# The attention steps of a fused conv-attention kernel: rows turned behind the normalised stream, the feed-forward product as four column tiles, the turn of the maxima ahead of the output product

## The chip, the cores and the metric

The kernel runs on one core of a Trainium2 chip. Its engines are TensorE (PE in the profile, with PEld for its weight loads), VectorE (DVE), ScalarE (ACT), GpSimd (POOL) and SyncE (SP), which issues most DMAs. They run their own instruction streams and wait for each other by semaphores. The metric is the device time of one execution in microseconds (us); the median of some runs is given, and one execution was recorded by the hardware profiler.

## The reference

The input x is 16 images of 64 x 64 positions with 128 channels (f32). One layer of three parts follows: a two-dimensional gated recurrence over the normalised image, an attention of the Nystrom kind over the 4096 positions of an image (8 heads of 16 channels, 64 landmarks), and a feed-forward recurrence along the positions. The part that matters here is the attention, with the first product of the feed-forward part:

```python
q_l = q.reshape(b, h, m, l, dh).mean(axis=3)          # landmarks: means over 64 positions
k_l = k.reshape(b, h, m, l, dh).mean(axis=3)
attn1 = softmax(q @ k_l.T); attn2 = softmax(q_l @ k_l.T); attn3 = softmax(q_l @ k.T)
out = attn1 @ pinv(attn2) @ (attn3 @ v) + conv33(v)
t = t + x + out @ w_out + b_out                       # x is the normalised stream
Wx = layer_norm(t) @ W.T                              # first product of the feed-forward part
```

(The lines are shortened; softmax, the 33-tap convolution along the positions and the pseudo-inverse are the reference's.)

## The kernel before, in words

The program has a stage of statistics, the two-dimensional recurrence (to about 1700 us of the span), the attention (to about 3400 us) and the feed-forward recurrence. Only the attention is touched.

**Tiling.** The attention works on groups of 512 positions: 8 groups make an image (Q = 8), 16 images make 128 groups. A group is 4 chunks of 128 positions (C = 4). One call of `step(s)` moves a software pipeline by one group: it handles different stages of groups that lie up to 20 apart. `new` is group s: its keys, values and queries are projected (L979, copied by ScalarE at L987, L997, L1007) and its scores against the landmark queries are taken (`greatest`, L1028), of which VectorE finds the maxima (`keep_greatest`, L1032, from bank 3 down to bank 0). `after` is group s + 1: the rows of the normalised stream are turned on TensorE into channels by positions (`turn_rows`, L960 on the tile at_xh) and copied by ScalarE (`keep_rows`, L968). `mid` is group s - 8, for which the weights against the landmark queries are made (`weigh`, L1058 and L1064; `weights`, L1073) and summed (`add_weights`, L1100 on GpSimd; `attend_values`, L1080). `first` is group s - 15: scores against the landmark keys (`compare`, L1135), their maxima (`topmost`, L1143), split into three bf16 parts by GpSimd (`part_top`, L1151 to L1154), turned (`turn_top`, L1159), copied (`keep_top`, L1163), and then used in `soften` (L1170 for the shift by the maxima, L1172 for the scores). `cur` is group s - 16: exponentials (`softened`, L1177), `attend` (L1184), the convolution (`convolve`, L1107), and `divide`: two transposes on VectorE (L1193), a reciprocal into PSUM (L1195) and a multiplication (L1197). `third` is group s - 17: output product (`output`, L1212) and sum (`keep_sum`, L1216). `fourth`, s - 18: mean and variance (`measure`, a statistics instruction L1225 and an aggregation L1226 for each chunk) and factors (on GpSimd). `fifth`, s - 19: normalised stream (`normalise`, L1238), its turn (`turn_output`, L960 on at_z, copied at L975), the feed-forward product (`feed`, L1244) and its copy, which also reorders the positions (`keep_feed`, L1248). `sixth`, s - 20: its statistics (L1252).

`step` runs for s = 15 to 127. Earlier steps have their own functions, and so have the steps after the last group (`last_step`); these are not changed. The first step of an image (`start`) has more to do: it gathers the sums of the image before and spreads its values.

**PSUM.** The results of TensorE go to PSUM, of which the program uses eight pieces of 512 f32 numbers in each partition, called banks. Six have numbers (`bank(k, ...)`, `banks(...)`), two are handed out as a pair. A bank has one tile at a time: an instruction that writes a new tile into a bank waits until the readers of the tile before are done. The numbers matter for the change: keys and `greatest` use bank 0, values bank 1, `greatest` banks 0 to 3, `weigh` 4, 5 and the pair, `turn_top` 2, `output` 3, `turn_output` 1, `attend` 4 and 5, the reciprocals of `divide` 2, `feed` 3, `turn_rows` 4, `attend_values` 5, `soften` 0 to 3, `compare` 4, 5 and the pair.

**Order.** In the attention the order on TensorE, VectorE, ScalarE and GpSimd is written out by hand (`tc.manual_schedule`): each engine executes in the order in which the functions of `step` are called. SP's queue of DMAs is ordered by the program's scheduler. Between the projection of the queries and the end of a step, the order of the calls is that of the diff below.

**Shapes of TensorE.** The profile gives a matmul's tile as rows x columns. The array can work as one tile of 128*128, as four tiles of 128*32 (four products for different columns of the output run side by side), of 32*128 (four products over different rows), or as eight of 64*32. `product` makes four products of 32 columns when `apart` is set:

```python
def product(out, lhsT, rhs, apart):
    for r in map(quarter, range(NP)) if apart else (slice(0, P),):
        nc.tensor.matmul(out[r], lhsT[:, r], rhs, start=True, stop=True)
```

An f32 product is two matmuls in the trace, one pass after the other.

Of the kernel before, what the change touches and what calls it, by code (L numbers as in the profile page):

```python
# [14 lines left out]
P = 128  # L15
# [830 lines left out]
def attention(nc, tc, t1, gamma, beta, wqkv, ident, mhalf, fixed, xp, rows, qm, km, pinvT, vd, t2, wx, wx_stats, out, ahead):  # L846
# [14 lines left out]
    C = 4  # L861
# [4 lines left out]
    BF = mybir.dt.bfloat16  # L866
    with ExitStack() as ctx:
# [7 lines left out]
        def bank(k, shape, dtype=F32):  # L875
            return ps.tile(shape, dtype, tag=f"bank{k}", name=f"at_bank{k}")
# [63 lines left out]
        def carry_factors(gr):  # L940
            gr.nbt = nb = sm.tile([P, 2, C], F32, tag="nb", name="at_nb")
            nc.gpsimd.tensor_tensor(nb[:, 1], gr.T[:, :, F], gr.T[:, :, F + 2], ALU.mult)
            nc.gpsimd.tensor_scalar(nb[:, 0], gr.T[:, :, F + 2], 1.0, None, ALU.add)
# [29 lines left out]
        def keep_output(gr):  # L973
            gr.zT = wk.tile([P, GC], F32, tag="zT", name="at_zT")
            nc.scalar.copy(gr.zT, gr.pz)  # L975
# [177 lines left out]
            nc.gpsimd.tensor_copy(top[:, :, 2:4], mx)  # L1153
            nc.gpsimd.tensor_tensor(top[:, :, 4:6], mx, top[:, :, 2:4], ALU.subtract)  # L1154

        def turn_top(gr):
            gr.pt = bank(2, [P, C, P], BF)
            for c in range(C):
                nc.tensor.transpose(gr.pt[:, c, :], gr.top[:, :, :, c].rearrange("p n s -> p (n s)"), ident_b)  # L1159

# [48 lines left out]
        def output(gr, k=3):  # L1209
            gr.po = bank(k, [P, C, F])  # L1210
            for c in range(C):
                nc.tensor.matmul(gr.po[:, c, :], gr.oT[:, c * P : (c + 1) * P], wo, start=True, stop=True)  # L1212
# [26 lines left out]
                    gr.z[:, c, :], gr.u[:, c, :], AF.Identity, bias=gr.nb[:, c : c + 1], scale=gr.r3[:, c : c + 1]  # L1239
                )  # L1240

        def feed(gr, k=3):
            (gr.pf,) = banks(k)
            nc.tensor.matmul(gr.pf, wfT, gr.zT, start=True, stop=True)  # L1244

        def keep_feed(gr):
            gr.fx = fx = wk.tile([P, GC], F32, tag="fx", name="at_fx")
# [152 lines left out]
        def step(s):  # L1400
            b, q = divmod(s, Q)
            new, after, mid, was = group(s), group(s + 1), group(s - Q), group(s - Q - 1)
            first, cur, third, fourth, fifth, sixth = (group(s - 2 * Q + d) for d in (1, 0, -1, -2, -3, -4))
            start = q == 0
            if first:
                compare(first)
            if cur:
                softened(cur)
            project_keys(new, apart=not start)
            if start:  # L1410
                sums(mid.im)
            project_values(new, apart=not start)
            if s == 2 * Q - 1:
                attend_values(was, 3)
                keep_values(was)
            if first:
                topmost(first)
            if sixth:
                measure_feed(sixth)
            if fourth:  # L1420
                measure(fourth, (0,))
            keep_keys(new)
            keep_projected(new)
            project_queries(new, apart=not start)
            if start and was:
                gather(was.im)
            if fourth:
                measure(fourth, (1,))
            keep_queries(new)
            if start:  # L1430
                turn_split(mid.im)
            if fifth:
                normalise(fifth)
            greatest(new)
            if first:
                carry_factors(first)
                carry(first, 2, nc.gpsimd)
            weigh(mid)
            keep_greatest(new)
            if first:  # L1440
                part_top(first)
            if third:
                output(third)
            weights(mid)
            if first:
                carry(first, 3, nc.gpsimd)
            if start and was:
                spread_values(was.im)
            if first:
                turn_top(first)  # L1450
            if fifth:
                turn_output(fifth)
                keep_output(fifth)
            if third:
                keep_sum(third)
            if fourth:
                measure(fourth, (2, 3))
            if cur:
                attend(cur)
            if first:  # L1460
                keep_top(first)
            add_weights(mid, (3, 1, 0), mid.g == 0)
            if fourth:
                factors(fourth)
            add_weights(mid, (2,))
            if q == Q - 1:
                shift(new.im)
            if cur:
                convolve(cur, pair())
                divide(cur)  # L1470
            if fifth:
                feed(fifth)
            if after:
                turn_rows(after)
            if fifth:
                keep_feed(fifth)
            if after:
                keep_rows(after)
            if first:
                carry(first, 0, nc.scalar)  # L1480
            attend_values(mid)
            if cur:
                add_convolved(cur)
            keep_values(mid)
            if first:
                soften(first)
                carry(first, 1, nc.scalar)
                carry_bias(first)
            if cur:
                turn_attended(cur)  # L1490
            fetch(s)
# [345 lines left out]
```

## Time and profile before

| What | us |
|---|---|
| median of 3 runs (lowest, highest) | 3635.04 (3631.91, 3635.63) |
| the profiled execution: its time, its span | 3638.43, 3636.9 |
| an ordinary step of the attention | 12.69 |
| the first step of an image | 15.79 |
| in the stretch 2400 to 2600: TensorE, VectorE, ScalarE, GpSimd busy of 200 | 199.1, 174.7, 163.2, 153.5 |

Times in the profile count from the first instruction. A step's length is the distance of the same instruction in two steps in a row. In the lists of instructions in order of time, a row merges instructions of a kind that follow each other: its first number is the start of the first, its second the time to the end of the last; the bracket, where there is one, gives idle time of the engine before it and what ended it. A matmul's end is modelled, and it is drawn with the time that its data takes through the array, so two matmuls in a row overlap; the distance of their starts is what one costs.

### The profile page before, as it was taken

Reading aid. Unit: us, or ns where it says so; the run is one execution under the profiler, and the core shown is the slowest. Engines: PE = TensorE matmul, PEld = TensorE weight load, DVE = VectorE, ACT = ScalarE, POOL = GpSimd, SP = SyncE. Lnnn points to the kernel's source line nnn. Section 1 sums busy time; section 2 is a strip of 40 time slices with the busy share of each in tenths; the row PEclk is TensorE's granted clock in tenths of the full one; section 3 lists DMA queues with packets and bytes.
Section 4 is the critical chain, followed back from the end, with each engine's and each line's share of the span. In section 5 each row is a group of like instructions: output and inputs, shape, how many; then the busy total and the mean of one; then the engine's idle time right before and its main releaser. Section 6 shows DMA issues by size and latency. Waiting matters only on the chain. (4 is left out here: it accounts for less than half of the span.)

```text
span 3636.9 us, 106193 instructions
## 1 busy us (share of the span) xinstructions
PE 3499.9 (96%) x40438; PEld 2343.7 (64%) x40438; DVE 2982.8 (82%) x7005; ACT 2499.9 (69%) x5126; POOL 2489.2 (68%) x3843
## 2 busy tenths in 40 slices
PE   7899999999999998999999999999999999997988
PEld 5666665545567666985666666666666666654777
DVE  8699999998889887544888888888888888888665
ACT  0466556656667665445788888888888888876787
POOL 1577877777788885434777777777777777785223
PEclk9999999999999999999999999999999999999999
DMA  9223232333333321023677777777777777667799
GB/s 339 83 76 80 80 86 80 84 84 83 85 88 86 81 76 38 4 63 92 147 185 187 164 162 163 166 167 163 164 166 166 165 164 168 157 143 187 201 273 182
DMA packets 834210, 484.50 MB, mean 133 GB/s; under 512 B 304672, under 2 KB 800672, under 8 KB 833696
## 3 DMA queue, kind: packets, MB, share of 16 engines
q1 hardware_dynamic: 814026, 442.55, 47.8%
q0 software_dynamic: 17728, 34.61, 5.3%
q8 instruction: 322, 5.28, 0.6%
q14 instruction: 192, 1.57, 0.1%
q10 hardware_dynamic: 1942, 0.50, 0.1%
HBM read 239.21 MB, written 238.29 MB: 131 GB/s over the span
## 5 line engine op out<-in xcount | busy, mean ns | idle before, releaser
L1100 POOL TENSOR_TENSOR at_total<-at_total,at_e 128x512 f32<-128x512 f32 x472 | 603.1, 1278 | 228.3 <-ACT at_e L1073 208.6
L290 ACT ACTIVATE ls_g<-ls_z,ls_b 128x304 f32<-128x304 f32 (+26 forms) x950 | 494.0, 545 | 225.0 <-PE ls_z L288 192.7
L283 PE MATMUL ls_z<-ls_xn,ls_w 128*128 128x432 f32 (+28 forms) x1700 | 586.1, 492 | 1.5 <-POOL ls_xn L275 1.2
L283 PEld LDWEIGHTS ls_z<-ls_xn,ls_w 128*128 128x128 f32 x1700 | 309.6, 191 | 189.4 <-issue 98.1
L288 PE MATMUL ls_z<-ls_hsum,ls_u 128*128 128x304 f32 (+26 forms) x1140 | 369.7, 461 | 0.0
L1032 DVE TENSOR_REDUCE at_mxq<-at_bank 128x1 f32<-128x512 f32 x512 | 314.9, 677 | 53.0 <-PE at_bank L1028 53.0
L323 POOL TENSOR_TENSOR ls_tt<-ls_ve,mhalf 128x8 f32<-128x8 f32 (+2 forms) x190 | 312.7, 1646 | 19.8 <-DVE ls_ve L322 4.2
L288 PEld LDWEIGHTS ls_z<-ls_hsum,ls_u 128*128 128x128 f32 x1140 | 211.6, 194 | 128.6 <-issue 78.4
L1177 ACT ACTIVATE at_eT<-at_bank 128x512 f32<-128x512 f32 x512 | 264.5, 604 | 42.1 <-PE at_bank L1172 41.5
L406 ACT ACTIVATE ls_g<-ls_cell 128x304 f32<-128x304 f32 (+26 forms) x190 | 93.2, 491 | 268.1 <-DVE ls_cell L405 267.8
L288 PE MATMUL ls_z<-ls_h,ls_u 128*128 128x304 f32 (+26 forms) x760 | 256.2, 460 | 12.3 <-DVE ls_h L410 12.3
L402 POOL TENSOR_TENSOR ls_g<-ls_g,ls_cell 128x304 f32<-128x304 f32 (+26 forms) x190 | 180.1, 948 | 127.7 <-ACT ls_g L290 113.0
L340 ACT ACTIVATE ls_tt<-ls_tt,ls_nb 128x128 f32<-128x128 f32 (+9 forms) x632 | 261.0, 478 | 5.6 <-POOL ls_tt L323 5.0
L979 PE MATMUL at_bank<-at_xT,wqkv 128*32 128x512 f32 (+1 forms) x1684 | 262.8, 602 | 2.0 <-DVE at_cmx L1143 1.1
L275 POOL TENSOR_TENSOR ls_xn<-ls_xn,grstd 128x272 f32<-128x272 f32 (+40 forms) x186 | 209.9, 1129 | 76.2 <-DVE ls_xn L270 71.2
L1143 DVE TENSOR_REDUCE at_cmx<-at_bank 128x8 f32<-128x512 f32 x256 | 175.6, 686 | 103.8 <-PE at_pair L1135 102.1
L1248 ACT COPY at_fx<-at_bank 128x512 f32<-128x512 f32 x128 | 133.7, 1044 | 142.9 <-PE at_bank L1244 138.3
L1619 DVE SCALAR_TENSOR_TENSOR rc_y<-rc_w,rc_scale,rc_z 128x256 f32<-128x256 f32 x344 | 154.6, 481 | 86.3 <-PE rc_z L1606 84.5
L1238 ACT ACTIVATE at_z<-at_u,at_nb,at_r 128x128 f32<-128x128 f32 x512 | 209.6, 484 | 4.6 <-POOL at_nb L1233 4.5
L288 PEld LDWEIGHTS ls_z<-ls_h,ls_u 128*128 128x128 f32 x760 | 141.9, 193 | 107.8 <-issue 53.2
L1600 POOL DMA_DIRECT2D out_dram<-rc_tt x64 | 77.4, 1209 | 168.4 <-ACT rc_tt L1597 145.0
L1193 DVE STREAM_TRANSPOSE at_t<-at_bank 128x512 f32<-128x512 f32 x256 | 167.9, 695 | 25.3 <-PE at_bank L1184 25.2
(281 smaller groups left out, 9683.8 us busy)
## 6 DMA issues: line engine op xcount, KB each, us to landing
at_win<-vd SPq DMA_DIRECT2D x256, 256.0 KB
t<-ls_tt SPq DMA_DIRECT2D x392, 130.0 KB
at_T<-t SPq DMA_DIRECT2D x128, 264.0 KB
gs_xb<-in_x_dram SPq DMA_DIRECT2D x64, 512.0 KB
at_xh<-t SPq DMA_DIRECT2D x128, 256.0 KB
vd<-at_v SPq DMA_DIRECT2D x128, 256.0 KB
t<-at_u SPq DMA_DIRECT2D x128, 256.0 KB
out_dram<-at_u SPq DMA_DIRECT2D x128, 256.0 KB
```

The costliest lines, as they stand in the source:

```text
L275: eng.tensor_tensor(a, a, norm(v, grstd), ALU.mult)
L283: nc.tensor.matmul(v.z[g][:, : v.total], wt[g], v.xn[:, : v.total], start=True, stop=True)
L288: nc.tensor.matmul(view(v, v.first.z[g]), ut[g], hin, start=False, stop=True, skip_group_check=True)
L290: nc.scalar.activation(a[:, : v.cols], z, AF.Tanh if g == 4 else AF.Sigmoid, bias=bt[g])
L323: nc.gpsimd.tensor_tensor(v.tt[:, 0:k, F + 2 : F + 4], ve[:, :, :k].rearrange("p r k -> p k r"), mhalf[:, : 2 * k].rearrange("p (k r) -> p ...
L340: nc.scalar.activation(v.tt[:q, k, F + 4 :], v.tt[:q, k, 0:F], AF.Identity, bias=v.nb[:q, k : k + 1], scale=v.tt[:q, k, F + 3 : F + 4],)
L402: nc.gpsimd.tensor_mul(v.a[1], v.a[1], v.cl)
L979: nc.tensor.matmul(out[r], lhsT[:, r], rhs, start=True, stop=True)
L1032: nc.vector.tensor_reduce(gr.im.mxq[:, n : n + 1, gr.g], gr.s[n], AX.X, ALU.max)
L1100: eng.tensor_tensor(total, total, e[:, :, c, :], ALU.add)
L1177: nc.scalar.activation(gr.eT[:, n], gr.s[n], AF.Exp)
L1238: nc.scalar.activation(gr.z[:, c, :], gr.u[:, c, :], AF.Identity, bias=gr.nb[:, c : c + 1], scale=gr.r3[:, c : c + 1])
```

## The change

In `step`, for all steps unless the condition says otherwise:

- `turn_rows(after)` goes ahead of `keep_sum(third)` and `attend(cur)`, directly behind `turn_output(fifth)`, and takes bank 0 instead of 4. `keep_rows(after)` goes behind `keep_top(first)`, ahead of `keep_feed(fifth)`.
- `feed(fifth)` makes four products of 32 columns instead of one of 128, still in bank 3.
- `part_top(first)` goes ahead of three other GpSimd operations of the same group.
- In steps that are not the first of an image: `turn_top(first)` goes ahead of `output(third)`; it takes bank 3, and the output bank 2. The statistics of chunk 1 of `fourth` go from ahead of the maxima (`keep_greatest`) to behind the output's sum (`keep_sum`).

No operation is added or left out but for the feed's products, of which there are four narrow ones in place of one.

```diff
-        def turn_top(gr):
-            gr.pt = bank(2, [P, C, P], BF)
+        def turn_top(gr, k=2):
+            gr.pt = bank(k, [P, C, P], BF)
...
-        def feed(gr, k=3):
+        def feed(gr, k=3, apart=False):
             (gr.pf,) = banks(k)
-            nc.tensor.matmul(gr.pf, wfT, gr.zT, start=True, stop=True)
+            product(gr.pf, wfT, gr.zT, apart)
...
-            if fourth:
+            if fourth and start:
                 measure(fourth, (1,))
             keep_queries(new)
...
             greatest(new)
             if first:
+                part_top(first)
                 carry_factors(first)
                 carry(first, 2, nc.gpsimd)
             weigh(mid)
             keep_greatest(new)
-            if first:
-                part_top(first)
+            if first and not start:
+                turn_top(first, 3)
             if third:
-                output(third)
+                output(third, 3 if start else 2)
             weights(mid)
...
-            if first:
+            if first and start:
                 turn_top(first)
             if fifth:
                 turn_output(fifth)
                 keep_output(fifth)
+            if after:
+                turn_rows(after, 0)
             if third:
                 keep_sum(third)
             if fourth:
-                measure(fourth, (2, 3))
+                measure(fourth, (2, 3) if start else (1, 2, 3))
             if cur:
                 attend(cur)
             if first:
                 keep_top(first)
+            if after:
+                keep_rows(after)
             add_weights(mid, (3, 1, 0), mid.g == 0)
...
                 convolve(cur, pair())
                 divide(cur)
             if fifth:
-                feed(fifth)
-            if after:
-                turn_rows(after)
-            if fifth:
+                feed(fifth, apart=True)
                 keep_feed(fifth)
-            if after:
-                keep_rows(after)
             if first:
                 carry(first, 0, nc.scalar)
             attend_values(mid)
```

## The prediction

> **What bounds the kernel now.** I read the page's header and its table of 40 slices first, then the busy time of the stretch in which the changed code runs, then the order of single instructions over one step, and last two steps in which the same order happens to be disturbed.
>
> ```profile
> span 3636.9 us, 106193 instructions
> PE 3499.9 (96%) x40438; PEld 2343.7 (64%) x40438; DVE 2982.8 (82%) x7005; ACT 2499.9 (69%) x5126; POOL 2489.2 (68%) x3843
> 1776.21:3175.93 1399.72, 1393.33 (x23629) 910.34 (x23627) 1222.77 (x2621) 1146.30 (x2274) 1083.55 (x1898) 1.00 0.72 167
> ```
>
> The third line is the stretch of the full attention steps: TensorE (first number after the length) is busy for 1393.33 of 1399.72 us at the full granted clock, VectorE for 1223. So a step's length is TensorE's: 12.69 us in the ordinary steps, 15.79 in the first step of an image. Whether a shorter TensorE program shortens the step depends on what comes ready just in time for it. One ordinary step, from the output product on (start, duration):
>
> ```profile
> 2411.83 1.16 PE L1212 MATMUL at_bank<-at_wo,at_oT 128*128 128x128 f32 x8
> 2412.83 0.39 PE L1159 MATMUL at_bank<-at_identb,at_top 128*128 128x128 bf16 x4
> 2413.05 0.61 PE L960 MATMUL at_bank<-ident,at_z 128*128 128x128 f32 x4
> 2413.58 1.09 PE L1184 MATMUL at_bank<-at_eT,at_g 64*32 64x512 f32 x16
> 2414.47 0.64 PE L1107 MATMUL at_pair<-at_win,bands 64*32 64x256 f32 x16
> 2414.76 1.31 DVE L1193 STREAM_TRANSPOSE at_t<-at_bank 128x512 f32<-128x512 f32 x2
> 2415.03 1.12 PE L1244 MATMUL at_bank<-at_zT,at_wfT 128*128 128x512 f32 x2
> 2416.00 0.60 PE L960 MATMUL at_bank<-ident,at_xh 128*128 128x128 f32 x4
> 2416.18 0.36 DVE L1195 RECIPROCAL at_bank<-at_t 128x32 f32<-128x32 f32 x1
> 2416.20 1.05 ACT L1248 COPY at_fx<-at_bank 128x512 f32<-128x512 f32 x1 [1.17 <-PE at_bank L1244]
> 2416.53 1.08 PE L1080 MATMUL at_bank<-at_e,at_v 128*32 128x128 f32 x32
> 2416.58 0.69 DVE L1197 TENSOR_TENSOR at_m<-at_t,at_bank 128x512 f32<-128x512 f32 x1
> 2417.54 0.40 PE L1170 MATMUL at_bank<-at_topT,at_minus 32*128 32x512 bf16 x4
> ```
>
> The reader is to see a race between `attend` (L1184) and `soften` (L1170). TensorE needs 3.96 us for it (2413.58 to 2417.54): attend, convolution, feed, the turn of the rows, values. Meanwhile VectorE must turn attend's two banks (L1193), take reciprocals into bank 2 (L1195) and multiply by them (L1197, end 2417.26), because the third product of L1170 writes bank 2. ScalarE must empty bank 3 (L1248, end 2417.24) for the fourth. VectorE's chain is 1.18 from attend's start to L1193, then 2.50 to the end of L1197, and 0.05 for the release: 3.73 us. Its margin to TensorE is only 0.23. What happens without the margin is shown by the last step, which has no rows left to turn:
>
> ```profile
> 3184.66 1.09 PE L1184 MATMUL at_bank<-at_eT,at_g 64*32 64x512 f32 x16
> 3185.84 1.31 DVE L1193 STREAM_TRANSPOSE at_t<-at_bank 128x512 f32<-128x512 f32 x2
> 3187.21 0.81 PEld L1080 LDWEIGHTS at_bank<-at_e,at_v 128*32 128x32 f32 x32 [0.80 <-DVE at_t L1193]
> 3187.66 0.69 DVE L1197 TENSOR_TENSOR at_m<-at_t,at_bank 128x512 f32<-128x512 f32 x1
> 3188.23 0.56 PE L1170 MATMUL at_bank<-at_topT,at_minus 32*128 32x512 bf16 x4
> ```
>
> There the values wait for L1193 to leave bank 5, and the four products of L1170 stretch over 0.56 instead of 0.40: the third starts at 3188.40, 0.05 after L1197 ends and again 3.73 after attend's start. That is the order of the changed kernel between attend and soften. A second disturbance: at 2430.23 the reciprocal came 0.35 late, the third product 0.12 later than its usual 0.007 behind the first, and that step became 12.84 us long instead of 12.69. So a late bank 2 goes into the step in full, and 0.03 on top (the four row tiles of soften run on out of step).
>
> **Part 1, turn_rows ahead of attend (bank 0).** Four transposes at 0.109 us apart, 0.437 in all, leave the path from attend to soften and stand between the turn of the stream and attend. On TensorE alone this is neutral or better: both turns are 128x128, so one change of tile shape goes. But attend starts 0.437 later, and with it VectorE's chain. New cover: none. Bank 0 is read last by the maxima (L1032), which end at about 2413.33; the turn is due at 2413.49, so it does not wait. Its copy (`keep_rows`, 0.77) moves into ScalarE's idle 1.17 before L1248 and is free; its reader is the next step's keys. The rows' load for a later group is issued earlier on SP; the buffers are two to three steps ahead, so I count nothing.
>
> **Part 2, the feed as four tiles of 32 columns, beside the values of the same shape.** From single instructions: after the last L1107 (2414.73, 0.21 long) the next weights start 0.09 after it has streamed, and L1244's two passes start 0.53 apart where 0.43 is the streaming, so 0.10 of weight load is exposed. Another 0.09 and 0.03 stand between the turn of the rows and L1080. The keys (L979, already apart) show 0.45 between their passes, and no gap follows where values and queries keep that shape. The saving is 0.10 - 0.02 + 0.09 + 0.01, about 0.18 us a step: TensorE alone would need 12.51. All of it lies between attend and soften, where TensorE then waits: its own way is 1.45 to the feed, 0.88 for it, 0.91 for the values, 0.09 for the change: 3.33 against VectorE's 3.73. So part 2 is worth nothing here. ScalarE's copy of the feed is next: the feed's last pass starts at attend + 1.92, L1248 follows 0.63 behind (2415.57 to 2416.20 now) and takes 1.05: end at 3.60, bank 3 free at 3.66, just inside 3.73.
>
> The row that the new order leans on is L1248: 1.05 us to empty one bank, however its product is made. The Trainium skill, TensorEngine Tiling (Array Packing), section Key Properties, says that changing the tiling mode drains the engine; that fits the 0.09 gaps. The same page, section PSUM Bottleneck, says that tiling speeds up the products but not the emptying of PSUM, which may become the limit; that speaks against this change. By the first rule alone the kernel would gain 0.18 x 109, some 20 us; by the second it gains none of that.
>
> **Part 3, the turn of the maxima ahead of the output product, banks 2 and 3 swapped.** The same twelve matmuls; the engine still changes shape once before them. Before, L1212's first weight load is exposed by 0.107 (0.213 between its first two starts, 0.11 later); now the bf16 load is exposed and half of the f32 load behind a 0.055 transpose: 0.055 + 0.05. I take 0, and bound it by all hidden and both exposed: -0.11 to +0.11. `part_top` moves ahead of three GpSimd operations and ends near 2411.07, before its turn at 2411.83. [...]
>
> **Part 4, measure 1 behind the output's sum.** VectorE's first maximum starts at 2410.92 now. L1028's last pass starts at 2410.20, and 0.68 (as from attend's last pass, 2414.08, to L1193) gives 2410.88: 0.04 sooner, no more. The output's last product starts at 2412.94 instead of 2412.71, so its sum (L1216) stays at 2413.3; three statistics of 0.41 behind 0.60 end at about 2415.12, where attend is ready for L1193 at 2415.20. Hidden, by 0.08.
>
> **The sum.** From soften's third product to the next attend is 8.73 us now. New step: 8.73 + 0.437 + 0.03 + 3.73 = 12.93, against 12.69: **+0.237 us**. Feed and rows both exist in 108 steps (numbers 19 to 126): +25.6 us. Of the steps before, the one whose soften starts at 1750.97 is already waiting (0.44), and the next has 0.34 to spare (0.10): +0.5. The first steps of images show the same margin (0.23) and are counted alike. The profiled execution, 3638.4 (span 3636.9), becomes 3664.5; it lies 3.4 over the median of the runs, 3635.04, so I forecast 3661 for the median. With part 3's bounds: 0.13 to 0.344 a step, 3650 to 3673.
>
> **Rivals.**
> - Faster: TensorE's program alone sets the step, -0.18 x 109 = -20 us, 3615. It needs VectorE's chain from attend to be 0.4 us shorter than 3.73, or bank 2 not needed; the last step speaks against it. TensorE's busy share and the removed shape change speak for it. It decides from the point where L1197 ends ahead of attend + 3.3.
> - No change: the late products of soften are made up behind it, or the maxima's turn saves its full 0.11 and the queue of weight loads another 0.1: 3635 to 3642. The disturbance at 2430 speaks against it.
> - Slower still: the three statistics end last, not attend. The added one is 0.41 to 0.46 and hidden by 0.08 only; with a sum that comes 0.1 to 0.2 later, 11 to 22 us come on top: 3672 to 3683. Two rows here speak for a close call, none for a later sum.
>
> **Chances.** Forecast 0.75 (3650 to 3673), slower still 0.09, no change 0.07, faster 0.09. The range 3642 to 3674 leaves the faster case, most of the slowest and half of no change out. By 0.2% (7.3 us, about what a measurement of this kernel can tell from no change): faster 0.09, same 0.07, slower 0.84.
>
> **What will show it.** Right: ordinary steps of about 12.93; L1193 starting 1.18 after attend; weight loads of L1080 waiting for DVE at_t; the third product of L1170 0.05 after L1197 and 0.15 to 0.2 behind the first; TensorE's busy time down by some 20 us while the span grows. Wrong: steps of 12.5 with L1170's four products within 0.02 (faster); L1193 with VectorE never idle before it and more than 1.25 after attend (slower still); an idle gap before the turn of the rows from L1032 (bank 0 late, a cost that I hold to be none).

## The result, and the profile after

| | before | after |
|---|---|---|
| median of 5 runs (lowest, highest), us | 3635.63 (3631.91, 3637.67) | 3671.18 (3670.26, 3676.87) |
| the profiled execution: its time, its span | 3638.43, 3636.9 | 3671.96, 3670.5 |
| ordinary step of the attention | 12.69 | 13.00 |
| first step of an image | 15.79 | 15.96 |

The ratio of the medians is 1.0099, with a 95% interval of 1.0086 to 1.0112: the changed kernel is slower by about 36 us. The forecast was 3661, its range 3642 to 3674. The direction and the place held, and so did the cause, VectorE's chain behind a later `attend`; which of its releases holds a step is less simple than the prediction had it (below). The forecast step was 0.07 us too short (12.93 for 13.00), and over the steps this is most of the 10 us by which the forecast missed.

The first two lines are the head of the page and its table of engines, for the changed kernel:

```profile
span 3670.5 us, 107432 instructions
PE 3525.2 (96%) x41092; PEld 2332.9 (64%) x41092; DVE 2994.0 (82%) x7005; ACT 2503.8 (68%) x5126; POOL 2491.3 (68%) x3843
```

TensorE's share is 96%, as before. By this line alone TensorE would look as busy as ever, and 25 us busier in sum, although by the prediction's estimate its program became shorter; the step below shows where its waits are hidden. The table of waits names them (engine and line that waited, for whom; us in total, times, longest):

```profile
PEld at_bank L1080 <- DVE at_t L1193: 110.0, 113, 1.6
ACT at_eT L1177 <- PE at_bank L1172: 84.1, 120, 3.2
DVE at_mxq L1032 <- PE at_bank L1028: 79.5, 127, 8.4
```

Before, no wait of L1080 stood among the thirty longest. Now the weights of the values wait 113 times, 0.97 us on average, for the transposes of VectorE: the wait that the prediction read off the last step. ScalarE and VectorE wait longer for TensorE too (before: 41.5 and 53.0), because all of them now stand in one ring: VectorE's chain from `attend` holds `soften`, and `soften` holds all that follows.

The same 107 steps that took 1399.72 us before take 1432.64 now (start:end of the stretch, its length, then busy times of TensorE, its loads, VectorE, ScalarE, GpSimd; granted clock, DMA share, GB/s):

```profile
1774.88:3207.52 1432.64, 1421.12 (x24272) 899.51 (x24269) 1234.46 (x2621) 1151.04 (x2275) 1085.52 (x1898) 1.00 0.69 164
```

That is +32.9 of the +33.6 us of the span, at the same granted clock of 1.00. VectorE has the same 2621 instructions and is busy 1234 instead of 1223 us. All but 0.7 us of the loss lies in these steps. One ordinary step of the changed kernel, in order of time (start, duration):

```profile
2399.29 0.41 PE L1159 MATMUL at_bank<-at_identb,at_top 128*128 128x128 bf16 x4
2399.66 1.16 PE L1212 MATMUL at_bank<-at_wo,at_oT 128*128 128x128 f32 x8
2400.65 0.60 PE L960 MATMUL at_bank<-ident,at_z 128*128 128x128 f32 x4
...
2401.09 0.60 PE L960 MATMUL at_bank<-ident,at_xh 128*128 128x128 f32 x4
2401.62 1.09 PE L1184 MATMUL at_bank<-at_eT,at_g 64*32 64x512 f32 x16
2402.82 1.29 DVE L1193 STREAM_TRANSPOSE at_t<-at_bank 128x512 f32<-128x512 f32 x2
2403.07 1.07 PE L979 MATMUL at_bank<-at_zT,at_wfT 128*32 128x512 f32 x8
2404.15 0.36 DVE L1195 RECIPROCAL at_bank<-at_t 128x32 f32<-128x32 f32 x1
2404.17 0.81 PEld L1080 LDWEIGHTS at_bank<-at_e,at_v 128*32 128x32 f32 x32 [0.94 <-DVE at_t L1193]
2404.20 1.05 ACT L1248 COPY at_fx<-at_bank 128x512 f32<-128x512 f32 x1 [1.05 <-PE at_bank L979]
2404.55 0.69 DVE L1197 TENSOR_TENSOR at_m<-at_t,at_bank 128x512 f32<-128x512 f32 x1
2405.18 0.49 PE L1170 MATMUL at_bank<-at_topT,at_minus 32*128 32x512 bf16 x4
```

The reader is to see three things. `attend` starts at 2401.62, with both turns (L960) ahead of it. The loads of the values wait 0.94 for L1193. And L1170 starts at attend + 3.56 but takes 0.49 instead of 0.40: the first two of its four products start at once, the third 0.05 after L1197 has ended (2405.24), the fourth 0.05 after L1248 has ended (2405.25). VectorE and ScalarE end within 0.02 of each other, at about attend + 3.62, where by the prediction's estimate TensorE's own program would need the banks at attend + 3.33.

Here is also why TensorE looks busy. L979's last product is drawn until 2404.14, with the time that its data takes through the array, and the values start at 2404.17. Alone, TensorE would have started them 0.88 after the feed, at 2403.95. The 0.22 of waiting lies under the drawn tail of the product before. The wait of the next paragraph, 0.11, lies under L1159's in the same way.

The first line hides the term that was mis-sized. Between L1159 and L1212 lie 0.37, where the four 0.055 transposes take 0.22. A step later, with the maxima and the weight loads beside them:

```profile
2411.31 2.48 DVE L1032 TENSOR_REDUCE at_mxq<-at_bank 128x1 f32<-128x512 f32 x4 [0.27 <-PE at_bank L1028]
2412.29 0.41 PE L1159 MATMUL at_bank<-at_identb,at_top 128*128 128x128 bf16 x4
2412.66 0.97 PEld L1212 LDWEIGHTS at_bank<-at_wo,at_oT 128*128 128x128 f32 x8
```

L1032 empties bank 3 first, then bank 2. Its four maxima start 0.60 apart and take 0.68 each, so the second ends at 2411.31 + 0.60 + 0.68 = 2412.59 (in the list of single instructions 2412.60). L1212 now writes bank 2, so its first weight load is let go at 2412.66, after the loading of weights has stood idle for 0.11. It then lies bare, as L1212's first load did before. Another 0.03 lies in the first bf16 load: L1159's first two products start 0.083 apart instead of 0.055.

### The profile page after: what moved, and what is told of

Its sections match the earlier page's. It is cut to its first block, busy times and chain, and to the rows that moved or that the text cites. A ratio compares the mean times of both kernels' runs of the same rounds, so it can differ in the third digit from the quotient of the medians.

```text
span 3670.5 us, 107432 instructions
## 1 busy us (share of the span) xinstructions
PE 3525.2 (96%) x41092; PEld 2332.9 (64%) x41092; DVE 2994.0 (82%) x7005; ACT 2503.8 (68%) x5126; POOL 2491.3 (68%) x3843
## 5 line engine op out<-in xcount | busy, mean ns | idle before, releaser
L1032 DVE TENSOR_REDUCE at_mxq<-at_bank 128x1 f32<-128x512 f32 x512 | 317.9, 683 | 79.5 <-PE at_bank L1028 79.5
L979 PE MATMUL at_bank<-at_xT,wqkv 128*32 128x512 f32 (+1 forms) x1684 | 262.6, 601 | 2.0 <-DVE at_cmx L1143 1.1
L1248 ACT COPY at_fx<-at_bank 128x512 f32<-128x512 f32 x128 | 134.5, 1051 | 126.6 <-PE at_bank L979 123.0
L1193 DVE STREAM_TRANSPOSE at_t<-at_bank 128x512 f32<-128x512 f32 x256 | 165.9, 686 | 34.0 <-PE at_bank L1184 34.0
```

The lines of the kernel that those rows point to most:

```text
L1032: nc.vector.tensor_reduce(gr.im.mxq[:, n : n + 1, gr.g], gr.s[n], AX.X, ALU.max)
```

## The experiments

Each kernel was timed beside the kernel before on one chip. The chip was another for rows 1 to 4, 5 to 8, 9 to 11 and 12, so the ratios are to be compared rather than the times. "Step" is the ordinary step; "stretch" the change of the 107 steps against 1399.7.

| kernel | time, us | ratio to before (95%) | step | stretch |
|---|---|---|---|---|
| part 1 alone | 3666.46 | 1.0073 (1.0059 to 1.0087) | 12.93 | +25.7 |
| part 2 alone | 3645.27 | 1.0023 (1.0014 to 1.0033) | 12.79 | +9.5 |
| part 3 alone | 3653.23 | 1.0039 (1.0025 to 1.0053) | 12.86 | +14.4 |
| part 4 alone | 3643.97 | 1.0018 (1.0009 to 1.0027) | 12.75 | +6.6 |
| after, part 3 undone | 3664.04 | 1.0070 (1.0057 to 1.0084) | 12.93 | +24.6 |
| after, reciprocals in SBUF | 3759.78 | 1.0338 (1.0325 to 1.0352) | 13.92 | +117.5 |
| the same, shorter copy of the feed | 3755.75 | 1.0330 (1.0316 to 1.0343) | 13.93 | +117.4 |
| parts 1 and 2, chains shortened, reciprocals in SBUF | 3682.31 | 1.0117 (1.0100 to 1.0134) | 13.13 | +39.0 |
| parts 1 and 2, chains shortened, reciprocals in bank 4 | 3623.16 | 0.9968 (0.9956 to 0.9980) | 12.50 | -13.3 |
| after, reciprocals in bank 4 | 3675.57 | 1.0122 (1.0106 to 1.0137) | 13.07 | +39.1 |
| the same, shorter copy of the feed | 3672.91 | 1.0109 (1.0093 to 1.0124) | 13.07 | +39.1 |
| before, chains shortened alone | 3634.90 | 1.0002 (0.9993 to 1.0011) | 12.71 | +2.5 |

### Each part alone

**Part 1 alone** (`turn_rows` and `keep_rows` moved, bank 0):

```diff
+            if after:
+                turn_rows(after, 0)
             if third:
                 keep_sum(third)
...
+            if after:
+                keep_rows(after)
             add_weights(mid, (3, 1, 0), mid.g == 0)
...
-            if after:
-                turn_rows(after)
...
-            if after:
-                keep_rows(after)
```

> Part 1 alone on the kernel before: the rows are turned ahead of attend (bank 0), their copy ahead of the feed's; the feed stays one product of 128 columns. Theory (the race): attend starts 0.437 later and VectorE's chain behind it (3.73 us to the release of bank 2) holds soften: an ordinary step of 12.93, about +26 us, 3661. Rival (TensorE's own program sets the step): the same products and the same number of shape changes, so 12.69 and 3635.

One step of it, in order of time:

```profile
2510.00 1.09 PE L1184 MATMUL at_bank<-at_eT,at_g 64*32 64x512 f32 x16
2511.18 1.31 DVE L1193 STREAM_TRANSPOSE at_t<-at_bank 128x512 f32<-128x512 f32 x2 [0.46 <-PE at_bank L1184]
2512.55 0.81 PEld L1080 LDWEIGHTS at_bank<-at_e,at_v 128*32 128x32 f32 x32 [0.80 <-DVE at_t L1193]
2512.99 0.69 DVE L1197 TENSOR_TENSOR at_m<-at_t,at_bank 128x512 f32<-128x512 f32 x1
2513.56 0.56 PE L1170 MATMUL at_bank<-at_topT,at_minus 32*128 32x512 bf16 x4
2514.39 0.28 DVE L1091 TENSOR_TENSOR at_sums<-at_bank,at_sums 128x128 f32<-128x128 f32 x1
2514.70 0.40 PE L1135 MATMUL at_bank<-km,at_QT 32*128 32x128 f32 x2
2515.83 1.07 PE L979 MATMUL at_bank<-at_xT,wqkv 128*32 128x512 f32 x8
```

L1193 starts 1.18 after attend, L1197 ends at 2513.68, and the third product starts 3.73 after attend. From the third product to the next attend lie 9.19, so the step is 9.19 + 3.73, measured 12.93: the forecast's sum to the hundredth. This part alone loses the race, and the time that leaves TensorE's program between attend and soften buys nothing. But bank 2 is not the only late bank here. VectorE's sum of the values (L1091), the last reader of bank 5, ends at 2514.67, and the next scores' second product, which writes bank 5, starts 0.055 later. The last experiment below shows that this second wait makes the step as long by itself.

**Part 2 alone** (the feed in four tiles, the rows still turned behind it):

```diff
-            nc.tensor.matmul(gr.pf, wfT, gr.zT, start=True, stop=True)
+            product(gr.pf, wfT, gr.zT, apart)
...
-                feed(fifth)
+                feed(fifth, apart=True)
```

> Part 2 alone: the feed as four tiles of 32 columns, the turn of the rows still behind it. Theory: the first weight load costs 0.08 less, but a shape change of 0.09 and an exposed load of 0.05 to 0.11 come between the feed and the turn of the rows, and the path from attend to soften is TensorE's here: 12.75 to 12.81, +6 to +13 us, 3641 to 3648. Rival (four tiles are the better product by themselves): -0.08 a step, 3627.

Measured: from attend to soften 4.05 instead of 3.96, step 12.79. The starts show where (medians): from the feed's start to the turn of the rows 1.00 (before 0.96), from there to the values 0.58 (before 0.53). Without part 1 the narrow products stand ahead of a 128*128 turn, and more is lost around the turn than the hidden load saves. That the changes of tile shape cost it is what the expectation said; no run separates them from the weight loads there.

**Part 3 alone** (the maxima's turn ahead of the output product, banks swapped):

```diff
+                part_top(first)
                 carry_factors(first)
...
-            if first:
-                part_top(first)
+            if first and not start:
+                turn_top(first, 3)
             if third:
-                output(third)
+                output(third, 3 if start else 2)
...
-            if first:
+            if first and start:
                 turn_top(first)
```

> Part 3 alone: the turn of the maxima ahead of the output product, banks 3 and 2 swapped, part_top earlier; the statistics of chunk 1 stay ahead of the maxima. Theory, formed on the changed kernel's trace: the output's first weight load waits for the second maximum, which empties bank 2; 0.15 to 0.21 a step in the 95 ordinary steps, 12.84 to 12.90, +14 to +20 us, 3649 to 3655. Rival (only weight loads are exposed differently, as the prediction had it): within 0.05 a step, 3630 to 3640.

One step of it:

```profile
2510.18 2.45 DVE L1032 TENSOR_REDUCE at_mxq<-at_bank 128x1 f32<-128x512 f32 x4
2511.10 0.41 PE L1159 MATMUL at_bank<-at_identb,at_top 128*128 128x128 bf16 x4
2511.49 0.97 PEld L1212 LDWEIGHTS at_bank<-at_wo,at_oT 128*128 128x128 f32 x8
```

The second maximum ends at 2510.18 + 0.59 + 0.68 = 2511.45; L1212's load follows 0.04 later, 0.39 behind L1159. In the median of the steps the load follows the end of the second maximum by 0.05 in this kernel and in the changed one, although both lie 0.02 further behind L1159 here: the load follows the maximum, and not the turn. The path from soften to attend grows from 8.73 to 8.89, and the step by the same 0.16. The first steps of images, where the order is the old one, keep their 15.79. So the cost comes with the new order and its banks: by the trace, 0.13 of waiting for the second maximum at bank 2 and 0.03 at the first bf16 load. No run has the new order with the old banks.

**Part 4 alone** (chunk 1's statistics behind the output's sum):

```diff
-            if fourth:
+            if fourth and start:
                 measure(fourth, (1,))
...
-                measure(fourth, (2, 3))
+                measure(fourth, (2, 3) if start else (1, 2, 3))
```

> Part 4 alone: the statistics of chunk 1 of the fourth group behind the output's sum instead of ahead of the maxima. Theory: the maxima start about 0.06 sooner, but L1193 comes 1.82 behind the sum's start instead of 1.48, 0.28 later than now, against a margin of 0.23 at bank 2: +0.05 to +0.08 a step in 95 steps, +5 to +8 us, 3640 to 3643. Rival (covered by attend): 3635.

One step of it, from attend on:

```profile
2515.93 1.09 PE L1184 MATMUL at_bank<-at_eT,at_g 64*32 64x512 f32 x16
2517.40 1.28 DVE L1193 STREAM_TRANSPOSE at_t<-at_bank 128x512 f32<-128x512 f32 x2
2519.18 0.69 DVE L1197 TENSOR_TENSOR at_m<-at_t,at_bank 128x512 f32<-128x512 f32 x1
2519.89 0.43 PE L1170 MATMUL at_bank<-at_topT,at_minus 32*128 32x512 bf16 x4
```

Here attend is not delayed, the third statistic pushes L1193 from attend + 1.18 to attend + 1.47, and that is just more than the margin of 0.23. The third product is 0.03 late, the step 0.06 longer.

The four stretches alone sum to 56.2 us, the four parts together cost 32.9. They are not additive. With part 1 no turn stands behind the narrow feed, so part 2 loses nothing there; part 3 gives 0.07 back on VectorE's chain (next experiment); and attend, 0.44 later, covers nearly all of part 4's third statistic.

**After, with part 3 undone** (the diff of part 3, reversed):

> The changed kernel without part 3: output, then the turn of the maxima, in banks 3 and 2, part_top behind the two other operations. Theory: the output no longer waits for the second maximum, so the twelve matmuls ahead of the turn of the stream cost 1.42 instead of 1.57; VectorE's chain gets its 0.09 wait for ScalarE at bank 2 back: 12.93 a step, -7 us, 3663. Rival (the order costs nothing once attend's race holds the step): 3671.

Measured 12.93 and 3664.04: 9.19 from the third product to attend, 3.73 from attend to it. L1193 is back at attend + 1.18, although part 4 is still in. Inside the changed kernel part 3 therefore costs 0.07 a step, not the 0.16 that it costs alone. The difference is a gift of the same swap. Before, the reciprocal's bank 2 had last been read by ScalarE; L1195 waits for ScalarE's semaphore besides VectorE's own, a semaphore instruction stands ahead of it in the trace, and it started 0.103 behind L1193. With the swap, bank 2 was last read by VectorE itself, the semaphore instruction is gone in the ordinary steps, and L1195 starts 0.034 behind. That takes 0.07 off VectorE's chain, which counts only where that chain ends last.

### Is it bank 2 that holds soften?

If VectorE's chain holds `soften` through the bank of the reciprocals, other memory for them should free it.

```diff
-            r = bank(k, [P, 2, NB])
+            r = sm.tile([P, 2, NB], F32, tag="rd", name="at_rd")
```

> The changed kernel, with the reciprocals of divide in SBUF instead of bank 2, so that soften's third product needs nothing of VectorE's chain. In the changed kernel's trace the fourth product starts 0.05 after ScalarE's copy of the feed ends as well. Theory (two chains end together, VectorE's at bank 2 and ScalarE's at bank 3): the fourth product stays where it is, 12.97 to 13.00 a step, 3667 to 3671. Rival (VectorE's chain alone holds soften): all four products start at attend + 3.56, -0.11 a step, 3658 to 3660.

A miss, and by far: 3759.78. The duration of the multiplication L1197 over the stretch (lowest/median/highest, ns), in the changed kernel and in this one:

```profile
L1197 DVE TENSOR_TENSOR at_m<-at_t,at_bank x103: 686/687/690, 1800.2 to 3167.9; 128x512 f32<-128x512 f32 x103
```

```profile
L1197 DVE TENSOR_TENSOR at_m<-at_t,at_rd x97: 712/1624/1645, 1806.0 to 3168.0; 128x512 f32<-128x512 f32 x97
```

With both operands in SBUF the same multiplication takes 1.62 us instead of 0.69. What runs beside it in one step:

```profile
2398.60 4.01 POOL L1100 TENSOR_TENSOR at_total<-at_total,at_e 128x512 f32<-128x512 f32 x3 [2.03 <-ACT at_e L1073]
2401.62 1.54 DVE L1197 TENSOR_TENSOR at_m<-at_t,at_rd 128x512 f32<-128x512 f32 x1
2402.27 0.40 PE L1170 MATMUL at_bank<-at_topT,at_minus 32*128 32x512 bf16 x4
```

GpSimd's additions, with two operands in SBUF themselves, end at 2402.61; the multiplication started at 2401.62 and ends at 2403.16, 0.55 after them. It looks as if it had stood for most of the time until GpSimd was through. The Trainium skill, SBUF — State Buffer, section Who interferes with whom, says that a VectorE instruction with two SBUF inputs contends with a GpSimd instruction that reads SBUF, that the port they share is an exclusive lock, and that the order of issue decides which of them blocks; these rows agree, with GpSimd's last addition begun before the multiplication. As for the question asked, the third product no longer waits for L1197, but the fourth still starts 0.05 after ScalarE's L1248: bank 3 holds `soften` just as well.

So the next kernel also shortens ScalarE's copy. The reorder of positions moves from the copy behind the feed to the one ahead of it:

```diff
-            nc.scalar.copy(gr.zT, gr.pz)
+            nc.scalar.copy(gr.zT.rearrange("p (l c) -> p c l", l=STEPS), gr.pz.rearrange("p (c l) -> p c l", l=STEPS))
...
-            nc.scalar.copy(fx.rearrange("p (l c) -> p c l", l=STEPS), gr.pf.rearrange("p (c l) -> p c l", l=STEPS))
+            nc.scalar.copy(fx, gr.pf)
```

> As the one before, and the reordering of positions is moved from the copy behind the feed product (1.05 us) to the copy in front of it, so that bank 3 comes free about 0.4 sooner and the longer copy lies in ScalarE's idle time; the same values are written. Theory: with both chains gone, soften starts all four products at attend + 3.56, held only by the values' wait for bank 5: -0.11 to -0.13 a step against the changed kernel, 3656 to 3660. Rival (the chains are not what holds soften, or the longer copy delays the feed by as much): 3670.

L1248 falls from 1.05 to 0.59, and all four products of L1170 start within 0.01 at attend + 3.56. The step stays at 13.93, since the multiplication is as slow as in the kernel ahead of it, and what VectorE empties behind it comes free late: the scores' second product starts at attend + 5.59, 0.055 after the sum of the values (L1091), where the first starts at 4.65 (medians).

### The race won

This kernel keeps parts 1 and 2, undoes 3 and 4, and shortens both chains: the shorter copy of the feed, the transposes with bank 5 first (the values wait for that one), the convolution copied out of its pair by ScalarE, and the values kept ahead of the sum of the convolution.

```diff
-            for j in range(2):
+            for j in (1, 0):
...
+            if aside:
+                cs = wk.tile([P, 2, GC // 2], F32, tag="cs", name="at_cs")
+                nc.scalar.copy(cs, at)
+                at = cs
...
+            keep_values(mid)
             if cur:
                 add_convolved(cur)
-            keep_values(mid)
```

> Parts 1 and 2 kept, parts 3 and 4 undone, and all of the race shortened: reciprocals in SBUF; the reordering in the copy ahead of the feed; attend's second bank (5) turned first by VectorE, so that the values need not wait; the convolution's result copied to SBUF by ScalarE, so that the pair of banks is free for the next scores, and the sum of the values ahead of the convolution's addition on VectorE, so that bank 5 is. Theory: TensorE's own way sets the step again and parts 1 and 2 give their 0.18: 12.51 to 12.60, 3616 to 3626. Rival (a further wait takes their place: ScalarE's extra copy of 0.6, or the banks of the next scores): 12.69 or more, 3635 and above.

Soften starts at attend + 3.32: the race is won. Yet most steps are 13.13 and the kernel is slower than before, a miss. The multiplication, still with both operands in SBUF, takes 1.74, and behind it the values' sum leaves bank 5 late for the next scores (one step of this kernel, whose lines from 1111 on are up to 4 further on: attend L1188, multiplication L1201, scores L1139):

```profile
2436.28 1.09 PE L1188 MATMUL at_bank<-at_eT,at_g 64*32 64x512 f32 x16
2439.21 1.74 DVE L1201 TENSOR_TENSOR at_m<-at_t,at_rd 128x512 f32<-128x512 f32 x1
2440.87 0.28 DVE L1091 TENSOR_TENSOR at_sums<-at_bank,at_sums 128x128 f32<-128x128 f32 x1
2441.20 0.18 PEld L1139 LDWEIGHTS at_bank<-km,at_QT 32*128 32x128 f32 x1 [0.34 <-DVE at_sums L1091]
```

The scores' second product starts at attend + 4.93, its first at 4.41.

Back into PSUM with the reciprocals, but into bank 4, which `soften` does not write:

```diff
-            r = sm.tile([P, 2, NB], F32, tag="rd", name="at_rd")
+            r = bank(k, [P, 2, NB])
...
-                divide(cur)
+                divide(cur, 4)
```

> As g4_race_won, but the reciprocals go to bank 4, which VectorE has itself emptied just before and which nobody needs until the next scores, instead of SBUF. In g4 the multiplication with both operands in SBUF took 1.74 us instead of 0.69 and ended with GpSimd's sum of the weights (2440.40), and bank 5 was late for the next scores by it; soften already came at attend + 3.32. Theory: with 0.69 back nothing is late, 12.51 to 12.60 a step, 3616 to 3626. Rival (the addition of the convolution, now with both operands in SBUF, waits for GpSimd in its turn and the output's operand is late): 12.7 and more, 3635 and above.

3623.16, faster than both kernels: 0.9968 of the kernel before. One step of it (its lines are 4 further on: attend L1188, transposes L1197, multiplication L1201, copy of the feed L1252, soften L1174):

```profile
2496.05 1.09 PE L1188 MATMUL at_bank<-at_eT,at_g 64*32 64x512 f32 x16
2497.25 1.31 DVE L1197 STREAM_TRANSPOSE at_t<-at_bank 128x512 f32<-128x512 f32 x2 [0.45 <-PE at_bank L1188]
2498.63 0.58 ACT L1252 COPY at_fx<-at_bank 128x512 f32<-128x512 f32 x1
2499.06 0.69 DVE L1201 TENSOR_TENSOR at_m<-at_t,at_bank 128x512 f32<-128x512 f32 x1
2499.37 0.40 PE L1174 MATMUL at_bank<-at_topT,at_minus 32*128 32x512 bf16 x4
```

Soften starts at attend + 3.32, while L1201 still runs (to 2499.75): it no longer stands between them. The step is 12.50, where the prediction had put TensorE's program alone at 12.51. So the faster rival's saving exists, and the changed kernel does not get it because two other engines end later. Against the 0.19 that an ordinary step gains, the first step of an image loses 0.13 (15.92) and the second 0.04 (12.73). In the first, TensorE stands idle for 0.51 until GpSimd's part of the shift is done (L1046), where the kernel before shows no idle time.

Is it the race, or do the shortened chains pay by themselves? The kernel before with the shortened chains alone (no part of the change; bank order and bank 2 as before):

> The kernel before with the shortened way of the race alone, without any of the four parts: the reorder in the copy ahead of the feed-forward, the convolution copied out of its pair by ScalarE, the values kept ahead of the sum of the convolution; the reciprocals stay in bank 2 and the banks keep their order. Theory: the step before is set by TensorE (3.96 us in the race against 3.73 of VectorE), so a shorter chain beside it brings nothing by itself: ordinary step 12.65 to 12.72, time 3632 to 3640, and the 10 us of the kernel that beat both come from rows turned ahead and the feed-forward in four tiles, once the chains are short enough. Rival: the shortened chains themselves gave the 10 us, through the bank and the pair that come free sooner: ordinary step 12.50 to 12.55, time 3618 to 3626.

Step 12.71, first step 15.89, time 3634.90: no difference. Chains that end 0.23 ahead of TensorE gain nothing by ending earlier still. Parts 1 and 2 paid only with the chains shortened, and these shortened chains not without parts 1 and 2. (Two of the fast kernel's edits are not in this one, bank 5 turned first and bank 4 for the reciprocals. Alone they have little to shorten: in the kernel before, soften and the values wait for neither bank.) Which of parts 1 and 2 brings how much of the 10 us was not tried.

### The changed kernel with the smallest repair

Bank 4 for the reciprocals as the only edit to the changed kernel (`divide(cur, 4)`):

> The changed kernel with one number changed: divide's reciprocals in bank 4 instead of 2. The repeat of g1 without its slow multiplication. Theory (ScalarE's copy of the feed at bank 3 holds the fourth product at the same time): 12.97 to 13.00 a step, 3667 to 3671. Rival (VectorE's chain alone holds soften): 12.88, 3657 to 3660.

The third product is free, the fourth waits for L1248 as before: ScalarE alone holds soften, as expected. Whether that sets the step is not shown, for the next kernel, without that wait, has the same 13.07. It is 0.07 longer than expected: the reciprocal again waits for ScalarE's semaphore too and starts 0.103 behind L1193, and the second product of the next scores (L1135, bank 5) comes 0.05 behind VectorE's sum of the values (L1091). With the shorter copy of the feed as well:

> As h2, and the reordering in the copy ahead of the feed, so that bank 3 comes free 0.4 sooner. Theory: both chains gone, all four products at attend + 3.56 behind the values' wait for bank 5: 12.87 to 12.90 a step, 3657 to 3660, still slower than the kernel before, since attend starts later. Rival (the longer copy ahead of the feed, or the sum of the values at bank 5, is late next): 13.00, 3670.

A miss against 12.87 to 12.90. One step of it:

```profile
2512.36 1.09 PE L1184 MATMUL at_bank<-at_eT,at_g 64*32 64x512 f32 x16
2514.91 1.08 PE L1080 MATMUL at_bank<-at_e,at_v 128*32 128x128 f32 x32
2515.92 0.39 PE L1170 MATMUL at_bank<-at_topT,at_minus 32*128 32x512 bf16 x4
2516.75 0.28 DVE L1091 TENSOR_TENSOR at_sums<-at_bank,at_sums 128x128 f32<-128x128 f32 x1
2517.01 0.45 PE L1135 MATMUL at_bank<-km,at_QT 32*128 32x128 f32 x2
2518.18 1.07 PE L979 MATMUL at_bank<-at_xT,wqkv 128*32 128x512 f32 x8
```

L1170 is clean at attend + 3.56, but the values' sum L1091, behind `divide` and the sum of the convolution on VectorE, ends at 2517.03, and the scores stretch behind it. VectorE's chain holds the step at three places: bank 5 by L1193, bank 2 by L1197, bank 5 again by L1091. Freeing one of them moves the wait to the next. The next keys (L979) start 5.82 after attend here, with soften clean, and 5.83 after it in part 1 alone, where soften's last two products were late. So there the late bank 5 is enough to make the step as long, and bank 2 is not shown to be what holds it. In the changed kernel itself L1091 ends 0.07 sooner, at attend + 4.61, and the scores' second product (4.66) hardly waits behind the first (4.65); the 0.07 that bank 4 costs is what brings this wait in. So what the changed kernel would take with soften free and the chain as short as it is was not measured.

## Why the prediction was right, and where it was off

- **The race (12.93).** Right in what loses it, VectorE's chain from attend, and in its length: part 1 alone gave 9.19 + 3.73 and 12.93 as summed. The margin of 0.23 was real: part 4 alone, which delays L1193 by 0.29, just oversteps it and costs 0.06 a step. But the prediction ended the chain at bank 2. It goes on to the sum of the values and bank 5, and that release makes a step of part 1 alone as long by itself. The last step before, from which the prediction read the race, had this wait as well (L1091 ends at 3189.33, the scores' second product starts at 3189.39). So the agreement to the hundredth is in part luck.
- **The late bank goes into the step in full, with 0.03 on top.** Right in size: part 1's 9.19 is 8.73 + 0.437 and 0.02. What the 0.02 is made of is open, since the scores wait for bank 5 on that path; in part 4 alone, where the scores do not wait for it, a third product 0.03 late costs the step 0.06.
- **Part 1: neutral for TensorE, no wait for bank 0.** Right: between the turn of the stream and attend stand 0.437 more and nothing else. In the changed kernel the turn of the rows has 0.29 to spare behind L1032; in part 1 alone it starts 0.04 late in four of the 103 steps.
- **Part 2: worth nothing here.** Right in the changed kernel, and 0.18 of TensorE's time appears as soon as the race is won (12.50 for 12.51). The saving lies where the prediction put it: from attend to soften 3.32, where before it was 3.96, less 0.44 for the turn of the rows, 3.52. How it divides between the feed and the moved turn was not tried. That L1248 ends at 3.60 and leaves bank 3 just inside 3.73 was right in kind and tighter than written: in the changed kernel both chains end within 0.02 of each other.
- **Part 3: "I take 0", bounds -0.11 to +0.11.** This is the mis-sized term. It measured +0.14 between the third product and attend (9.33 for 9.19) and +0.16 alone. The working counted which weight load lies bare and where the bf16 load hides, but not who had last read the output's new bank. Bank 2 is emptied by the second maximum, 0.60 behind the first. The same swap gives back 0.065 of VectorE's chain (3.73 forecast, 3.67 measured), through the reciprocal that need not wait for ScalarE's semaphore. Net 0.07 a step; the stretch with part 3 undone is 8.3 us shorter: the greater part of the 10 us that the forecast lacks. Some 2.6 us are of another kind: the forecast took off 3.4 because the profiled execution lay so far above the median, and of the changed kernel it lay only 0.8 above.
- **Part 4: "hidden, by 0.08".** Right without part 3: with that undone, L1193 starts at attend + 1.18 in the ordinary steps and in the last steps of images (the one at s = 127, with no rows to turn, aside). In the changed kernel part 3's late output uses the margin up. VectorE stands idle for 0.21 before the output's sum (L1216), which the prediction had held in its place, and the statistics end last by 0.02 (L1193 at 1.20); in the last step of an image, where VectorE also has L1037 (0.15), L1193 starts at 1.27 and the step is 13.08. The step at s = 127, 12.30 before, became 13.08; it was not forecast. So the rival "three statistics end last" is in part what happened: the sum comes 0.15 later, within the 0.1 to 0.2 of its condition, and the statistics end last by 0.02 in ordinary steps and by 0.09 in one step of eight.
- **TensorE's busy time "down by some 20 us".** Wrong: the page shows 25 us more, because waits lie under the drawn tails, as said with the step after.
- **Faster rival.** It fails in this kernel for the reason given, and of its conditions (L1197 ahead of attend + 3.3, or bank 2 not needed) the fast kernel met the second; L1197 still ends at attend + 3.70 there. It needed more than that: ScalarE's bank 3 and VectorE's sum of the values as well, neither of which the rival named.
- **The page on tiling.** The Trainium skill, TensorEngine Tiling (Array Packing), section PSUM Bottleneck, says that tiling speeds up TensorE but not the emptying of PSUM. The runs agree: L1248 takes 1.05 behind the four tiles as behind the one product, and with bank 4 it holds soften's fourth product by itself. The kernel at 12.50 has it at 0.58, beside the other shortened chains; no run has that kernel with the long copy. Of the 0.18 that the prediction put down to changes of shape alone, 0.08 is weight load by its own terms.

What stays open: which late bank holds the step of part 1 alone, bank 2 or bank 5; what part 3 costs with the new order and the old banks; the first two steps of images in the fast kernel; and the shares of parts 1 and 2 in its gain.

## What to carry to other kernels

Before moving work out of a stretch of the busiest engine, list for each bank that is written at the end of the stretch, and for some way behind it, who empties it and when, counted from the start of the stretch; the gain is at most the smallest of those margins, however many instructions are moved. A release that is shown to be late is not yet the one that holds the step: free it, and see whether the step becomes shorter. A tile that changes its bank gets new predecessors: look up the last reader of the new bank and the order in which it reads, even if the product itself costs the same. And a busy share of 96% before and after did not tell which engine sets the step; the order of single instructions in one step did.

## What the runs showed of the hardware

- A 128x512 f32 multiplication on VectorE took 0.69 us with one operand in PSUM and 1.62 to 1.74 us (medians) with both in SBUF, beside GpSimd's additions of SBUF operands. The sum of the convolution behaves alike: 0.69 with the convolution in PSUM, 0.87 and 0.79 (medians, up to 1.39) in the two kernels that had copied it to SBUF and were no slower than before; in the third, behind the slow multiplication, 0.68.
- ScalarE's copy of 128x512 f32 out of PSUM took 1.05 us with the reorder and 0.59 without. The reorder was not free elsewhere: the copy ahead of the feed rose from 0.62 to 1.07. It only moved off the path.
- A reciprocal that waits for ScalarE's semaphore as well as VectorE's own, with a semaphore instruction of its own ahead of it, started 0.103 us after the transposes, although ScalarE had long been done; waiting for VectorE's own alone it started after 0.034.
- One late product among four side by side cost more than its lateness. In the changed kernel with bank 4 and the shorter copy, the scores' second product came 0.08 us late and the next keys 0.19 (5.83 after attend, where 4.65 + 0.99 is 5.64; 0.99 is the scores' length in the kernel before).
